# Two key loads moved from GpSimd's queue to SyncE's, and a graph part interleaved from an earlier point of an MLP

## The chip, the cores and the metric

The kernel runs on one core of a Trainium2 chip. The metric is the device time of one execution in microseconds; each kernel is run several times and the median is given. All arithmetic is in float32, apart from a small comparison buffer in bfloat16.

The engines are named as the profile names them: PE (TensorE, matmuls), PEld (its weight loads), DVE (VectorE), ACT (ScalarE), POOL (GpSimd), SP (SyncE, which here issues transfers only). "SPq" is SP's own queue of instructions. Each engine works through its instructions in order; a transfer (DMA) is issued by an engine and moves on its own afterwards.

## The reference, cut to what matters

One layer of a graph network on 1250 nodes with 768 features. A graph attention block and a linear-attention block with an MLP read the same normalized input and are added; a mixture of two chosen experts follows.

```python
xn = layernorm(x)
x = x + gnn(xn, edges) + mix(xn)            # both need xn only
x = x + ffn(layernorm(x))                   # 2 of 4 experts

def gnn(x, edges):                          # 21250 edges with the self loops
    out1 = gat(layernorm(x), W1, 4 heads)   # softmax over the edges into a node
    out2 = gat(out1, W2, 2 heads)
    return concat(x, out2) @ Wu + bu

def mix(x):
    x = x + linear_attention(layernorm(x))
    return x + gelu(layernorm(x) @ fc1) @ fc2   # 768 -> 3072 -> 768
```

## The kernel before

**The graph as a dense table.** Attention over edges is computed with a dense 1250 x 1250 table of edge counts in DRAM. There are two such tables (`tabs[0]`, `tabs[1]`), which are cleared with large transfers on SP's queue near the start (`clear`, L208). Each edge becomes a key, source times 1250 plus destination. The 21250 keys are written to DRAM (`key_d`) and taken in ten pieces of 17 columns of 125 edges. For each piece the keys are loaded again, one copy on every partition (`kr` for the first four pieces, `kr_l` for the later six), DVE compares them with the column of keys (`eq`, L295), counts duplicates (L300, L305) and computes where each count goes (`place`, L308 to L313). Then POOL issues 17 indirect transfers (L315) that add the counts into the tables, column c into `tabs[c % 2]`: 170 in all.

**The four early pieces.** They are put between the row tiles of the first matmul stage (`ps_u`, L545): piece 0 after tile 1, piece 1 after tile 3, piece 2 after tile 5, piece 3 after tile 7. `edge_piece(i)` also issues the load of piece i + 2 into one of two buffers, so that load must wait until the comparison of piece i has read its buffer. The loads of pieces 0 and 1 are issued on POOL before that stage. The later six pieces load over SP (L334).

**The stages in order of time.** Folded weights, then `ps_u` (to about 116 us), the graph's first features `ps_g` (to about 200), keys, values and queries of the linear attention (to about 440), its projection `ps_p` (L974, to about 521), then the mix MLP from about 521 to 1335, and the two experts to the end.

**The mix MLP.** It runs over 12 groups `g` of 256 hidden columns, and in each over two sets of columns `c`. The work of a group is cut in steps "P" (three matmuls of the first layer in the Strassen form, `fc1_unit`) and "h" (half a row tile of the second layer, `fc2_half`: two matmuls into a bank `ps_f`, L1077, then one DVE addition into the accumulator, L1082). There are three banks for `ps_f`. The halves done in one column set are those whose hidden values were computed in the one before. The order is written out as two strings:

```python
for c, pattern in enumerate(("PPhhhhPhhPPhhPPhhhh", "PPhhPhhPPhhPPhh")):
```

**The graph's part in the MLP.** The generator `gnn()` is the whole rest of the graph block, cut in steps that each yield a cost in us. `spend(us)` is called after each "P" (1.36 in the first column set, 2.04 in the second) and each "h" (1.39); it adds to a credit, and while the credit covers the cost of the step before, the next step is issued. What is left at the second column set of the last group is issued in one go (L1401).

The first step of `gnn()`, in `largest(4, ...)`, issues on POOL the additions of the second table to the first for the first three of ten row blocks (`merged`, L1115) and the loads of row blocks 0 and 1 of the sum (`fetch`, L1128), and yields 9.0. All of these come behind the last indirect addition into the tables. The next step begins with DVE's reading of row block 0: a `far` instruction (L1143) and then one running maximum per head (L1151 in block 0, L1147 in the others), two heads per step, cost 5.0 each. These DVE instructions are pinned (`pin`) behind what was traced before them on their engine. Unpinned instructions, such as those of the MLP, may be issued in an order other than that of the text where the program's builder finds them ready sooner.

Of the kernel before, what the change touches and what calls it, by code (L numbers as in the profile page):

```python
# [32 lines left out]
def tile_gps_layer(ctx, tc, a, out):  # L33
    nc = tc.nc
# [5 lines left out]
    def bcast(ap, p):  # L40
        return ap.partition_broadcast(p)
# [231 lines left out]
    def load_keys(i, engine):  # L273
        c0 = i * PIECE
        kr = ep.tile([128, PIECE, TP], F32, name="kr", bufs=2)
        engine.dma_start(
            kr, bcast(key_row[c0 * TP : (c0 + PIECE) * TP], 128).rearrange(
                "p (c e) -> p c e", e=TP
            ),
        )  # L280
        keys[i] = kr

    def edge_steps(i, pool, kr, parts):

        c0 = i * PIECE
        eq = pool.tile([TP, PIECE, TP], BF16, name="eq", bufs=2)
        for n in range(3):
            at = 0  # L290
            for w in parts[n]:
                cs, ks = slice(at, at + w), slice(c0 + at, c0 + at + w)
                at += w
                if n == 0:
                    pin(nc.vector.tensor_tensor(  # L295
                        eq[:, cs], kr[:TP, cs],
                        kcol[:, ks].unsqueeze(2).to_broadcast([TP, w, TP]), ALU.is_equal,
                    ))
                elif n == 1:
                    nc.vector.tensor_tensor(  # L300
                        eq[:, cs], eq[:, cs],
                        counts_of[:TP].unsqueeze(1).to_broadcast([TP, w, TP]), ALU.mult,
                    )
                else:
                    nc.vector.tensor_reduce(mult[:, ks], eq[:, cs], AX.X, ALU.add)  # L305
                yield n
        first = pool.tile([TP, PIECE], F32, name="first", bufs=2)
        nc.vector.tensor_scalar(first, mult[:, c0 : c0 + PIECE], 256.0, None, op0=ALU.is_lt)  # L308
        at = pool.tile([TP, PIECE], F32, name="at_e", bufs=2)
        nc.vector.scalar_tensor_tensor(  # L310
            at, kcol[:, c0 : c0 + PIECE], trash, first, op0=ALU.subtract, op1=ALU.mult
        )
        nc.vector.tensor_scalar(place[:, c0 : c0 + PIECE], at, trash, None, op0=ALU.add)  # L313
        for c in range(c0, c0 + PIECE):
            nc.gpsimd.indirect_dma_start(  # L315
                out=tabs[c % 2][:, :],
                out_offset=bass.IndirectOffsetOnAxis(ap=place[:, c : c + 1], axis=0),
                in_=mult[:, c : c + 1], in_offset=None,
                bounds_check=TABLE - 1, oob_is_err=True, compute_op=ALU.add,
            )  # L320

    def edge_piece(i):
        kr = keys.pop(i)
        if i + 2 < SOON:
            load_keys(i + 2, nc.gpsimd)
        for _ in edge_steps(i, ep, kr, ((PIECE,),) * 3):
            pass

# [207 lines left out]
    for t in range(NT):  # L536
        tc_ = slice(t * TP, (t + 1) * TP)
        if t + 1 < NT:
            normalized(t + 1)
        for c0, w in HALVES:  # L540
            if c0 and t + 1 < NT:
                turned_x(t + 1)
            ps = bank("ps_u")
            for k in range(KC):
                nc.tensor.matmul(  # L545
                    ps[:TP, :w], fT[:, k, tc_], wu[:, k, c0 : c0 + w],
                    start=k == 0, stop=k == KC - 1,
                )
            o = acc[:, t, c0 : c0 + w]
            nc.vector.tensor_tensor(o, ps[:TP, :w], o, ALU.add)  # L550
        for t0, n in SPLITS[1:]:
            if t == t0 - 2:
                for t1 in range(t0, t0 + n):
                    moments(acc[:, t1, :], mv[:, t1, :], vec)
                scales(t0, n)
        if t == 8:
            ahead = norms(0)
        if t in pieces:
            edge_piece(pieces[t])
# [335 lines left out]
    with tc.tile_pool(name="qp", bufs=1) as qp:  # L895
# [70 lines left out]
        for part in order2:  # L966
# [27 lines left out]
            for t in part:  # L994
                z = qp.tile([TP, D], F32, name="z2", bufs=2)
                i = where[t]
# [364 lines left out]


    steps = gnn()
    credit, cost = -44.0, 0.0

    def spend(us):
        nonlocal credit, cost
        credit += 1.05 * us
        while cost is not None and credit >= cost:
            credit -= cost  # L1370
            cost = next(steps, None)
# [15 lines left out]
    def put_half(g, c, t, j):  # L1387
        fc2_half(g, c, t, j)
        spend(1.39)
        if g == GROUPS - 1 and j:  # L1390
            last_tile(t)

    todo = []
    for g in range(GROUPS):
        if g:
            load_fc1(g + 1)
            load_fc2(g, 1)
            load_fc2(g + 1, 0)
        for c, pattern in enumerate(("PPhhhhPhhPPhhPPhhhh", "PPhhPhhPPhhPPhh")):
            if g == GROUPS - 1 and c:  # L1400
                for _ in steps:  # L1401
                    pass
                cost = None
                gnn_pool.__exit__(None, None, None)
            parts = fc1_unit(g, c)
            for p in pattern:
                if p == "P":
                    next(parts)
                    if g or c:
                        spend(2.04 if c else 1.36)  # L1410
                elif todo:
                    put_half(*todo.pop(0))
            todo = halves_of(g, c)
# [447 lines left out]
```

## Time and profile before

| | us |
|---|---|
| median of 3 runs | 1904.69 (1903.83 to 1906.24) |
| the profiled execution: its own time | 1900.13 |
| its span, first to last instruction | 1898.2 |
| PE busy | 1869.0 (98%) |
| DVE busy | 1336.0 (70%) |
| ACT busy | 803.3 (42%) |
| POOL busy | 498.0 (26%) |

PE is busy for 98% of the span, so the time is the sum of PE's work and of the few gaps in it. The shares are means over stages; where a gap lies is read from the waits of PE and from a table by stretches of time. In the timelines a line gives start, duration, engine, source line, operation, and in brackets how long the engine had been idle and what ended that.

### The profile page before, as it was taken

What the parts mean: (1) busy time and instruction counts of PE and PEld (TensorE: products, weight loads), DVE (VectorE), ACT (ScalarE), POOL (GpSimd) and SP (SyncE); (2) the same over time, 40 slices, a digit from 0 to 9 for tenths busy, and PEclk for the clock granted to TensorE, in tenths of its full rate; (3) what the DMA queues carried; (4) which work ended last, traced back from release to release, by engine and by line L of the source; (5) the groups of instructions that cost most, each with busy time, mean ns of one, the idle gap of its engine ahead of it and who ended that gap; (6) DMA issues with size and microseconds to landing.
All of it is one profiled execution on the core that took longest, in us unless ns stands there. A gap on an engine that the chain in (4) does not pass through costs nothing.

```text
span 1898.2 us, 19544 instructions
## 1 busy us (share of the span) xinstructions
PE 1869.0 (98%) x6966; PEld 1245.7 (66%) x6966; DVE 1336.0 (70%) x2407; ACT 803.3 (42%) x1207; POOL 498.0 (26%) x341
## 2 busy tenths in 40 slices
PE   9999999999998999999999999999999999999998
PEld 7555556865565668787777655566766666666664
DVE  4656692677546967676666977766677777777778
ACT  3233221331321128777674186645364353433330
POOL 2265766687882110111111121000221000000000
PEclk9999999999998999999999999999999999999999
DMA  9748532523139751233343532202485201011023
GB/s 341 238 97 213 114 85 52 134 19 49 2 30 187 136 145 55 70 95 88 106 113 79 151 111 73 69 9 67 126 101 82 71 0 67 3 64 47 12 87 109
DMA packets 184285, 175.50 MB, mean 92 GB/s; under 512 B 110043, under 2 KB 153595, under 8 KB 182908
## 3 DMA queue, kind: packets, MB, share of 16 engines
q0 software_dynamic: 126640, 68.01, 20.8%
q1 hardware_dynamic: 54270, 98.48, 16.4%
q10 hardware_dynamic: 3278, 7.75, 1.3%
q8 instruction: 55, 0.90, 0.2%
q14 instruction: 42, 0.34, 0.1%
HBM read 137.80 MB, written 42.05 MB: 95 GB/s over the span
## 4 chain that ended last, share of the span: by engine, by line
PE 91%; DMA 4%; POOL 1%; DVE 1%; issue 1%; ACT 1%; SPq 0%; DVEq 0%; POOLq 0%; ACTq 0%
PE ps_f L1077 14%; PE ps_p L81 13%; PE ps_r L81 12%; PE ps_o L1255 7%; PE ps_a L127 7%; PE ps_g L578 4%; PE ps_u L545 4%; PE ps_p L974 4%; PE ps_c L127 3%; PE ps_f L1655 3%; PE ps_o L1294 2%; PE ps_va L127 2%; PE ps_ka L127 2%; PE ps_qa L127 2%; PE ps_d L127 2%; POOL tab L315 1%
## 5 line engine op out<-in xcount | busy, mean ns | idle before, releaser
L315 POOL DMA_INDIRECT tab<-mult,place_e x170 | 351.1, 2065 | 157.7 <-DMA tab<-mult,place_e 102.6
L1077 PE MATMUL ps_f<-w,v 128*125 128x384 f32 x960 | 338.9, 487 | 6.9 <-DVE slot_a L1082 6.9
L1077 PEld LDWEIGHTS ps_f<-w,v 128*125 128x125 f32 x960 | 178.0, 188 | 113.4 <-DVE slot_a L1082 8.0
L1082 DVE TENSOR_TENSOR slot_a<-ps_f,slot_a 125x384 f32<-125x384 f32 x240 | 131.6, 553 | 66.6 <-PE ps_f L1077 62.7
L1210 DVE TENSOR_TENSOR wt<-ee 125x375 f32<-125x375 f32 (+1 forms) x180 | 105.9, 590 | 84.5 <-PE ps_o L1255 57.5
L1255 PEld LDWEIGHTS ps_o<-turns,wt 125*125 125x125 f32 x800 | 137.1, 188 | 29.1 <-DVE wt L1211 4.0
L1255 PE MATMUL ps_o<-turns,wt 125*125 125x193 f32 x800 | 151.7, 329 | 2.9 <-DVE wt L1211 2.9
L1205 ACT ACTIVATE ee<-bt,s 125x375 f32<-125x375 f32 (+1 forms) x180 | 114.8, 638 | 77.1 <-DVE wt L1210 69.8
L81 PE MATMUL ps_p<-fT,w 128*128 128x312 f32 (+1 forms) x432 | 125.5, 426 | 0.6 <-ACT c L1573 0.6
L1211 DVE SCALAR_TENSOR_TENSOR wt<-wt,slot_x 125x375 f32<-125x375 f32 (+1 forms) x180 | 105.9, 590 | 4.4
L81 PEld LDWEIGHTS ps_p<-fT,w 128*128 128x128 f32 x432 | 81.5, 189 | 36.2 <-ACT c L1573 1.1
L81 PE MATMUL ps_r<-w,slot_a 128*125 128x384 f32 x260 | 94.5, 486 | 0.0
L127 PE MATMUL ps_a<-fT,w 128*128 128x250 f32 (+1 forms) x288 | 86.8, 432 | 0.7 <-DVE slot_a L979 0.7
L1617 DVE SCALAR_TENSOR_TENSOR slot_x<-ps_r,gate,slot_x 125x384 f32<-125x384 f32 x100 | 60.7, 615 | 33.3 <-PE ps_r L81 33.0
L81 PE MATMUL ps_p<-xt,ws 128*128 128x313 f32 (+1 forms) x288 | 83.6, 426 | 0.0
L578 PE MATMUL ps_g<-fx,zT 128*125 128x388 f32 x240 | 80.2, 490 | 1.5 <-DVE zT L372 1.5
L545 PE MATMUL ps_u<-wu,fT 128*125 128x384 f32 x240 | 79.9, 487 | 0.4 <-ACT fT L531 0.4
L974 PE MATMUL ps_p<-wp,slot_x 128*125 128x384 f32 x240 | 79.9, 486 | 0.0
L1147 DVE SCALAR_TENSOR_TENSOR slot_x<-turns,s,slot_x 125x1250 f32<-125x1250 f32 x54 | 79.4, 1512 | 0.1
L1026 ACT ACTIVATE v<-v,par 128x250 f32<-128x250 f32 (+1 forms) x72 | 40.0, 556 | 88.0 <-DVE v L1046 41.3
L1208 ACT ACTIVATE ee<-bt,s1l 125x375 f32<-125x375 f32 (+1 forms) x120 | 75.4, 628 | 0.1
L81 PE MATMUL ps_r<-w2s,ht 128*125 128x384 f32 x200 | 72.7, 486 | 0.0
(403 smaller groups left out, 3413.0 us busy)
## 6 DMA issues: line engine op xcount, KB each, us to landing
turns<-g_d POOLq DMA_DIRECT2D x12, 942.4 KB, 14.2
w<-in_L_mix_fc_w_dram SPq DMA_DIRECT2D x12, 768.0 KB
w<-in_L_mix_fc_w_dram SPq DMA_DIRECT2D x24, 384.0 KB
slot_x<-tab POOLq DMA_DIRECT2D x14, 610.4 KB, 6.6
w<-in_L_ffn_w_dram SPq DMA_DIRECT2D x11, 768.0 KB
w<-in_L_ffn_w_dram SPq DMA_DIRECT2D x5, 1536.0 KB
slot_x<-tab POOLq DMA_DIRECT2D x40, 183.1 KB, 3.3
kr_l<-key_d SPq DMA_DIRECT2D x6, 1062.5 KB
```

The lines of the kernel that those rows point to most:

```text
L81: return lambda *args, **kw: pin(getattr(self.engine, name)(*args, **kw))
L127: engine.matmul(ps, wt[:, k, :], x[:, k, :], start=k == 0 and not more, stop=k == n - 1, skip_group_check=more,)
L315: nc.gpsimd.indirect_dma_start(out=tabs[c % 2][:, :], out_offset=bass.IndirectOffsetOnAxis(ap=place[:, c : c + 1], axis=0), in_=mult[:, c ...
L545: nc.tensor.matmul(ps[:TP, :w], fT[:, k, tc_], wu[:, k, c0 : c0 + w], start=k == 0, stop=k == KC - 1,)
L578: nc.tensor.matmul(ps[:TP, :388], zT[:, k, :], fx[:, k, h2 * 388 : (h2 + 1) * 388], start=k == 0, stop=k == KC - 1,)
L974: nc.tensor.matmul(ps[:TP, :w], qT[:, k, t * TP : (t + 1) * TP], pm[:, k, c0 : c0 + w], start=k == 0, stop=k == KC - 1,)
L1077: nc.tensor.matmul(ps, v_of[c][:, f, h, at : at + TP], lasts[g, j][:, f, :], start=f == 0, stop=f == 1,)
L1082: nc.vector.tensor_tensor(o, ps, o, ALU.add)
L1205: nc.scalar.activation(e[:, 0, :w], bt[:TP, 0, :w], AF.Exp, bias=s[:, 0, h, c : c + 1])
L1210: nc.vector.tensor_tensor(wt[:, :w], e[:, 0, :w], e[:, 1, :w], ALU.max)
L1211: nc.vector.scalar_tensor_tensor(wt[:, :w], wt[:, :w], 1.0, adj, op0=ALU.min, op1=ALU.mult)
L1255: nc.tensor.matmul(sums[i // 2][:TP, (i % 2) * 193 : (i % 2 + 1) * 193], wt[:, i * TP : (i + 1) * TP], gh[:, c, :], start=c == 0 and i % 2 ...
```

## The change

Two edits. The loads of pieces 2 and 3 of the keys are issued by SP instead of POOL. The credit of the interleaving begins at -20 instead of -44, and each "P" or "h" adds 1.01 times its cost instead of 1.05 times.

```diff
     def edge_piece(i):
         kr = keys.pop(i)
         if i + 2 < SOON:
-            load_keys(i + 2, nc.gpsimd)
+            load_keys(i + 2, nc.sync)
...
     steps = gnn()
-    credit, cost = -44.0, 0.0
+    credit, cost = -20.0, 0.0
 
     def spend(us):
         nonlocal credit, cost
-        credit += 1.05 * us
+        credit += 1.01 * us
         while cost is not None and credit >= cost:
             credit -= cost
             cost = next(steps, None)
```

## The prediction, made before the change was run

> **What bounds the kernel now.** I read the waits of PE first, because PE is busy 98% of the span: only its gaps can be won, and any new gap is paid in full.
>
> ```profile
> PE ps_f L1077 <- DVE slot_a L1082: 6.9, 1, 6.9
> PE ps_o L1255 <- DVE wt L1211: 2.9, 1, 2.9
> ```
>
> The largest gap lies in the mix MLP and waits for a DVE addition. The table by stretches of time (length; busy time of PE, PEld, DVE, ACT, POOL; granted clock; DMA share; GB/s) shows that the rest of the MLP has next to nothing to win:
>
> ```profile
> 580.00:600.00 20.00, 13.14 (x36) 7.33 (x35) 9.40 (x13) 1.44 (x3) 6.56 (x6) 0.78 1.22 204
> 600.00:700.00 100.00, 100.00 (x366) 65.91 (x366) 90.31 (x120) 13.80 (x28) 17.90 (x21) 0.99 0.72 141
> 700.00:720.00 20.00, 17.09 (x54) 11.15 (x53) 7.74 (x15) 13.48 (x15) 2.14 (x4) 0.91 0.41 139
> 720.00:900.00 180.00, 180.00 (x834) 144.25 (x834) 128.60 (x268) 141.71 (x208) 24.14 (x26) 1.00 0.29 79
> ```
>
> Even at 90% DVE, PE is full from 600 to 700. Next the DVE timeline around the gap, to see what the addition stood behind:
>
> ```profile
> 557.72 0.42 DVE L1046 TENSOR_TENSOR v<-ps_d,c 128x250 f32<-128x250 f32 x1 [1.71 <-PE ps_d L127]
> 558.94 0.56 DVE L1082 TENSOR_TENSOR slot_a<-ps_f,slot_a 125x384 f32<-125x384 f32 x1 [0.80 <-PE ps_f L1077]
> ...
> 579.46 0.56 DVE L1082 TENSOR_TENSOR slot_a<-ps_f,slot_a 125x384 f32<-125x384 f32 x1 [0.73 <-PE ps_f L1077]
> 590.54 0.96 DVE L1143 TENSOR_SCALAR turns<-slot_x 125x1250 f32<-125x1250 f32 x1 [10.53 <-DMA slot_x<-tab]
> 591.54 1.74 DVE L1151 TENSOR_SCALAR slot_x<-turns,s 125x1250 f32<-125x1250 f32 x2
> 593.21 0.53 DVE L1046 TENSOR_TENSOR v<-ps_d,c 128x375 f32<-128x375 f32 x1
> 593.67 1.64 DVE L1151 TENSOR_SCALAR slot_x<-turns,s 125x1250 f32<-125x1250 f32 x2
> 595.23 1.01 DVE L1082 TENSOR_TENSOR slot_a<-ps_f,slot_a 125x384 f32<-125x384 f32 x2
> ```
>
> DVE stands 10.5 us in front of the first `far` (L1143), waiting for row block 0. PE ran on until the three `ps_f` banks were full:
>
> ```profile
> 562.61 1.43 PE L127 MATMUL ps_a<-xt,ws 128*128 128x250 f32 x6
> 563.87 2.74 PE L1077 MATMUL ps_f<-w,v 128*125 128x384 f32 x8
> ...
> 587.51 1.45 PE L1077 MATMUL ps_f<-w,v 128*125 128x384 f32 x4
> 595.83 2.92 PE L1077 MATMUL ps_f<-w,v 128*125 128x384 f32 x4 [6.86 <-DVE slot_a L1082]
> 598.54 3.52 PE L127 MATMUL ps_a<-fT,w 128*128 128x375 f32 x6
> ```
>
> Last, the chain of waits, for what row block 0 itself waits for:
>
> ```profile
> 560.30 3.61 DMA tab<-mult,place_e
> 565.37 17.10 DMA tab<-tab
> 583.19 9.14 DMA slot_x<-tab
> ```
>
> The last of 170 indirect additions goes out at 560.30; then three merges and two loads follow, and the block lands at 590.5. That date hangs on POOL's additions, not on where DVE asks for it. DVE already asks too early.
>
> **Second edit: the earlier start.** Counting the costs along the two strings: the first `far` falls due when the credit covers 9.0. Before: (9 + 44) / 1.05 = 50.5 us of counted work, reached with the last "h" of group 1, column set 0 (25.4 for group 0, 26.2 for this set: 51.6). That is the addition at 579.46 above, and `far` is the very next DVE instruction, so the trace follows the text. After: (9 + 20) / 1.01 = 28.7, reached with the first "h" of the same set (25.4 + 2 x 1.36 + 1.39 = 29.5): the addition at 558.94. `far` moves 20.5 us forward in DVE's queue.
>
> With row block 0 still landing at 590.54:
> - DVE waits from 559.50 instead of 580.02: +20.5.
> - The cover shrinks. Before, PE ran on from 580.02 to 588.96 (587.51 + 1.45), 8.9 us. After, behind the first "h" stand three halves (three banks), one P (562.61) and then a half whose bank only DVE can free: PE stops at 563.87, 4.4 us after DVE. +4.5.
> - Behind `far` only two heads come before the next addition (0.96 + 1.7 = 2.7 us), where before four heads and an L1046 did (590.54 to 595.23, 4.7 us): -2.0.
>
> Sum +23.0: a PE gap of about 30 us instead of 6.9. Queued behind `far` on DVE are the additions of halves 2 to 4 and all later MLP work; PE waits for the first of them.
>
> SP's two weight loads at 566.64 and 579.45 are released by PE's progress, so they now fall behind the stall and no longer share the engines with the merges (the DMA share is 1.22 in 580 to 600). Between 0 and 3 us of gain; I take 1.5, about their share of the traffic: -1.5.
>
> **The clock after the stall.** Behind the gap four matmuls took 2.92 us instead of 1.45 and six 3.52 instead of 2.05: 2.9 us lost to the lower clock (0.78 in that stretch), in a kernel that already has it. The Trainium skill, "TensorE: Matmul & The Clock Gate", section "What's actually happening", says that the clock falls to half after an idle window of about 3.4 us and returns after one busy one, however long the idle was: 1.7 us as an estimate, against 2.9 measured. By the row the change costs nothing here, by the rule up to 1.2 us less. The row stands: 0.
>
> **What the slower rate is worth.** The generator's costs sum to 536. It ends at (536 + 44) / 1.05 = 552 before and (536 + 20) / 1.01 = 550 after, both short of the 567.6 counted before the last column set: no leftover is issued at once in either. DVE's load between falls by 4%, but PE is idle only some 3.8 us from 600 to 1335, 2.9 of it a wait for a transfer (`b_d`, then `bt`) that keeps the same steps around it. Bounds 0 to -3; I take 0.
>
> **First edit: the keys over SP.** On POOL it removes two issues:
>
> ```profile
> 52.27 0.53 POOL L276 DMA_DIRECT2D kr<-key_d  x1 [30.65 <-DVE eq L295]
> 57.18 2.12 POOL L315 DMA_INDIRECT tab<-mult,place_e  x1 [4.38 <-DVE place_e L313]
> 71.38 2.00 POOL L315 DMA_INDIRECT tab<-mult,place_e  x1 [12.08 <-DMA tab<-mult,place_e]
> ...
> 100.49 1.40 POOL L276 DMA_DIRECT2D kr<-key_d  x1
> ```
>
> The first issue lies in time in which POOL waits for `place` anyway: 0. The second frees 1.7 us (1.40 and 0.30 of issue). The first six additions, 57 to 102, wait for one another's landing while SP's loads and clears fill the engines; without a key load ahead, the first may land sooner (13.3 us after its issue, the next 11.5): -1.8.
>
> A rule of the Trainium skill speaks against more. "DMA: Bandwidth & Descriptors", section "Issuing engines are not separate DMA queues": transfers from all engines run on the same 16 DMA engines and interleave; another issuer saves only the time to initiate. By the rule the additions end 1.7 us sooner, no more. The trace can be worse: SP's key load at 179.45 is followed by additions that wait 3.10 and 3.41 us (182.36, 187.75). SP reaches the two loads behind its other loads, at 76 to 84, beside additions 2 to 5; two loads at some 3 us are +6. Against this the load at 100.49 no longer stands in front of its additions: -2. Sum -1.7 - 1.8 + 6 - 2, about 0, between -6 and +6. It moves row block 0, and so the end, one for one: from 360 on POOL issues an addition every 2.3 us almost without waits and absorbs nothing. By the rule the total would be 1.7 lower; I take 0.
>
> On SP two issues are added (0.3 us each by the `kr_l` loads). They wait for `eq` of pieces 0 and 1 (done at 52.0 and 68.7), earlier than SP gets there; behind them stands the `wk` load, which waits for PE until 116: 0. If the keys of piece 2 land late (90 to 95), DVE waits up to 6 us at 89.2 instead of 6.5 at 100.5 as now; six banks cover it, since PE is busy 83.92 of 84 us from 32 to 116. Without that cover, 6.
>
> **Sum.** 23.0 - 1.5 + 0 + 0 = +21.5 on the profiled execution's 1900.13: 1921.6. The median of the runs stands 4.6 us over that execution: 1926.2.
>
> **The rivals.**
> 1. *It is faster.* The six additions from 57 to 102 take 45 us; at 2.3 us each they would take 14. If the keys are what holds them, row block 0 lands up to 31 us sooner, DVE stands free, and the old gap goes too: -6.9 - 2.9, 1894.9. The deciding point is row block 0 at about 567: 23 us sooner it breaks even. Against it: only one of the six follows a key load; the others wait just as long. 0.05.
> 2. *`far` doesn't move as far.* MLP additions are not pinned, and the builder can let ready ones pass (L114 of the next weights ran at 553.00, before the L1046 at 557.72 that precedes it in the text). Then DVE stalls less: +3 to +14, about 1913. Against it: at 580 no ready L1046 passed `far`. 0.09.
> 3. *The keys on SP hold the additions more than counted*, 8 to 12 us: 1935 to 1939. 0.06.
>
> The rest, 0.80, is the forecast; its own range is 1917 to 1936 (scatter -6 to +6, loads and later waits -3 to +3). A difference under 0.2%, 3.8 us, can't be told from none here. Rival 1 gives faster 0.05; a little of rival 2 falls within 0.2%: same 0.04; slower 0.91. The range 1915 to 1936 leaves out rival 1, most of rival 2 and rival 3.
>
> **What the profile after would show.** Right: L1143 first waits about 30 us for `slot_x<-tab`, behind an L1082 near 559; PE's wait for L1082 is near 29 us as one gap; the last L315 is still at 554 to 567; 600 to 1335 without new waits. Wrong: the last L315 before 545 (rival 1), or L1046 and L1082 running between 560 and 590 (rival 2). A `wt` or `ee` wait grown by several us in 700 to 1335 would mean that the slower rate isn't neutral.

## The result, and the profile after

The changed kernel takes 1918.34 us, the median of 5 runs (1915.76 to 1918.56), against 1904.69 for the kernel before (5 runs, 1901.2 to 1907.02). The ratio is 1.0072 [1.0056, 1.0088]: 13.65 us slower. The profiled execution after took 1918.45 with a span of 1916.6, so the pair of profiled executions differs by 18.3. Why these two differ is taken up at the end of the explanation below.

The waits of PE after the change (total, times, longest, in us). The largest has grown from 6.9 to 32.5, in one piece. The wait at the first `ps_o` (L1255, 2.9 before) is not in the list any more; the one at L1294 is of the later two-head layer.

```profile
PE ps_f L1077 <- DVE slot_a L1082: 32.5, 1, 32.5
...
PE ps_o L1294 <- DVE wt L1211: 1.4, 2, 1.2
```

The DVE timeline after. The first `far` (L1143) now stands behind the addition at 558.87 and not behind that at 579.46, and DVE waits 35.68 us in front of it. The line after `far` is new too: an addition of the MLP, which is not pinned, comes ahead of the running maxima (L1151).

```profile
557.64 0.42 DVE L1046 TENSOR_TENSOR v<-ps_d,c 128x250 f32<-128x250 f32 x1 [1.71 <-PE ps_d L127]
558.87 0.56 DVE L1082 TENSOR_TENSOR slot_a<-ps_f,slot_a 125x384 f32<-125x384 f32 x1 [0.80 <-PE ps_f L1077]
595.10 0.88 DVE L1143 TENSOR_SCALAR turns<-slot_x 125x1250 f32<-125x1250 f32 x1 [35.68 <-DMA slot_x<-tab]
595.90 0.54 DVE L1082 TENSOR_TENSOR slot_a<-ps_f,slot_a 125x384 f32<-125x384 f32 x1
596.37 1.64 DVE L1151 TENSOR_SCALAR slot_x<-turns,s 125x1250 f32<-125x1250 f32 x2
```

The PE timeline after. PE goes on for one P (562.53) and stops near 563.97, three halves and a P behind the addition, as the count of the banks said. The first eight matmuls behind the gap take 4.48 us, where eight took 2.74 in the kernel before (563.87).

```profile
557.38 5.32 PE L1077 MATMUL ps_f<-w,v 128*125 128x384 f32 x16
562.53 1.43 PE L127 MATMUL ps_a<-xt,ws 128*128 128x250 f32 x6
596.50 4.48 PE L1077 MATMUL ps_f<-w,v 128*125 128x384 f32 x8 [32.53 <-DVE slot_a L1082]
600.81 1.43 PE L127 MATMUL ps_a<-fT,w 128*128 128x250 f32 x6
```

The chain of waits after. The last addition into the tables goes out at 564.92, before at 560.30, and the row block lands 4.6 us later (595.10 against 590.54). From one to the other it takes 30.2 us in both.

```profile
564.92 3.65 DMA tab<-mult,place_e
...
569.08 4.59 DMA tab<-tab
...
580.00 15.08 DMA slot_x<-tab
...
595.10 0.88 DVE turns L1143
```

The table by stretches after. In 560 to 600 PE is busy for 7.47 us, where it was 33.14 before. From 600 to 900 there is nothing left to win: 700 to 720 is full, where the kernel before had 17.09 of 20.

```profile
560.00:600.00 40.00, 7.47 (x21) 4.37 (x20) 4.90 (x8) 0.37 (x1) 15.68 (x12) 0.62 0.94 110
580.00:600.00 20.00, 3.50 (x6) 1.97 (x7) 4.90 (x8) 0.00 (x0) 5.09 (x5) 0.50 1.21 169
600.00:700.00 100.00, 100.00 (x368) 65.73 (x367) 92.87 (x117) 13.80 (x28) 19.06 (x21) 1.00 0.74 144
700.00:720.00 20.00, 20.00 (x79) 14.09 (x79) 10.33 (x23) 8.07 (x14) 3.07 (x5) 1.00 0.53 163
720.00:900.00 180.00, 180.00 (x823) 142.66 (x822) 126.71 (x259) 136.05 (x199) 22.51 (x23) 1.00 0.28 78
```

### The profile page after: what moved, and what is told of

Read it like the earlier page. It is cut to its first block, busy times and chain, and to the rows that moved or that the text cites. A ratio compares the mean times of both kernels' runs of the same rounds, so it can differ in the third digit from the quotient of the medians.

```text
span 1916.6 us, 19550 instructions
## 1 busy us (share of the span) xinstructions
PE 1863.1 (97%) x6966; PEld 1241.4 (65%) x6966; DVE 1338.3 (70%) x2407; ACT 806.9 (42%) x1209; POOL 496.0 (26%) x339
## 3 DMA queue, kind: packets, MB, share of 16 engines
q0 software_dynamic: 126352, 65.84, 20.5%
## 4 chain that ended last, share of the span: by engine, by line
PE 85%; POOL 5%; issue 5%; DMA 2%; DVE 1%; ACT 1%; ACTq 0%; SPq 0%; DVEq 0%; POOLq 0%
PE ps_f L1077 15%; PE ps_p L81 13%; PE ps_r L81 12%; PE ps_a L127 7%; PE ps_o L1255 7%; POOL tab L315 5%; PE ps_u L545 4%; PE ps_c L127 3%; PE ps_g L578 3%; PE ps_f L1655 3%; PE ps_o L1294 2%; PE ps_va L127 2%; PE ps_ka L127 2%; PE ps_d L127 2%; PE ps_u L1307 1%
## 5 line engine op out<-in xcount | busy, mean ns | idle before, releaser
L315 POOL DMA_INDIRECT tab<-mult,place_e x170 | 349.9, 2059 | 195.0 <-DMA tab<-mult,place_e 119.7
L1077 PE MATMUL ps_f<-w,v 128*125 128x384 f32 x960 | 339.3, 488 | 32.5 <-DVE slot_a L1082 32.5
L1082 DVE TENSOR_TENSOR slot_a<-ps_f,slot_a 125x384 f32<-125x384 f32 x240 | 132.0, 553 | 58.1 <-PE ps_f L1077 53.9
L1205 ACT ACTIVATE ee<-bt,s 125x375 f32<-125x375 f32 (+1 forms) x180 | 115.0, 639 | 90.7 <-DVE wt L1210 84.7
L1255 PEld LDWEIGHTS ps_o<-turns,wt 125*125 125x125 f32 x800 | 136.2, 187 | 25.9 <-issue 0.8
L1255 PE MATMUL ps_o<-turns,wt 125*125 125x193 f32 x800 | 149.6, 326 | 0.0
L1208 ACT ACTIVATE ee<-bt,s1l 125x375 f32<-125x375 f32 (+1 forms) x120 | 75.4, 629 | 0.1
L1026 ACT ACTIVATE v<-v,par 128x250 f32<-128x250 f32 (+1 forms) x72 | 40.0, 555 | 73.6 <-DVE v L1066 28.3
```

What stands on the lines that cost most here:

```text
L315: nc.gpsimd.indirect_dma_start(out=tabs[c % 2][:, :], out_offset=bass.IndirectOffsetOnAxis(ap=place[:, c : c + 1], axis=0), in_=mult[:, c ...
L1077: nc.tensor.matmul(ps, v_of[c][:, f, h, at : at + TP], lasts[g, j][:, f, :], start=f == 0, stop=f == 1,)
L1082: nc.vector.tensor_tensor(o, ps, o, ALU.add)
L1205: nc.scalar.activation(e[:, 0, :w], bt[:TP, 0, :w], AF.Exp, bias=s[:, 0, h, c : c + 1])
L1255: nc.tensor.matmul(sums[i // 2][:TP, (i % 2) * 193 : (i % 2 + 1) * 193], wt[:, i * TP : (i + 1) * TP], gh[:, c, :], start=c == 0 and i % 2 ...
```

## The experiments

The theory: the loss is `far` asking 20.6 us earlier for a row block whose date is set by POOL's 170 additions, and nothing else in the change matters much. The rivals: the keys on SP delay the additions; or the slower rate makes new waits later in the MLP. A second question came up on the way: what the right place for `far` is. The kernels ran on four chips, each chip with its own runs of the kernel before, and each ratio is against those. The kernel before has medians of 1897.46, 1906.61, 1906.92 and 1904.76 on the four, so a ratio from one chip is not to be compared closely with one from another.

### One edit at a time

The keys alone:

```diff
-            load_keys(i + 2, nc.gpsimd)
+            load_keys(i + 2, nc.sync)
```

> Only the keys of pieces 2 and 3 over SP; credit as before (-44, 1.05). Theory A (row block 0's landing sets when DVE may go on, and the keys on SP make the additions end later): last L315 near 565 as in the changed kernel (before: 560.3), PE's gap at L1082 about 6.9 + 4.6 = 11.5 us, time +3 to +6 over before. Theory B (the key loads are free, the later end in the changed kernel is scatter of the runs): last L315 at 558 to 562, time within 2 us of before. Theory C (POOL freed, additions end sooner): L315 before 558, time 0 to -5.

Measured: 1902.2 (22 runs), ratio 1.0018 [1.0002, 1.0033]. The profile has `far` at 593.00 behind a wait of 12.73, and a PE gap of 9.1, against 590.54, 10.53 and 6.9: the shape of the kernel before, with a table 2.5 us later and a time 3.0 longer (1903.13).

The credit alone:

```diff
-    credit, cost = -44.0, 0.0
+    credit, cost = -20.0, 0.0
...
-        credit += 1.05 * us
+        credit += 1.01 * us
```

> Only the credit (-20, 1.01); keys over POOL as before. Theory A: last L315 near 560.3, far (L1143) still right behind the L1082 at 559, DVE waits about 31 us and PE about 28 (32.5 in the changed kernel less 4.6), time +10 to +16 over before, about 4 below the changed kernel. Theory B (the keys count for nothing): the same time as the changed kernel, +13 to +15. Theory C (most of the loss comes from the keys): +0 to +5.

Measured: 1912.71 (7 runs), ratio 1.0091 [1.0057, 1.0125]. The shape of the kernel after is here without the keys, in the waits of PE and in the DVE timeline:

```profile
PE ps_f L1077 <- DVE slot_a L1082: 25.4, 1, 25.4
```
```profile
589.11 0.88 DVE L1143 TENSOR_SCALAR turns<-slot_x 125x1250 f32<-125x1250 f32 x1 [28.56 <-DMA slot_x<-tab]
```

The whole change once more, beside others on a second chip:

> The changed kernel once more, beside the kernel before and on the chip of the experiments. Theory A (the two edits add up: keys +3.4, credit +17.3 by e1_keys and e2_credit): +18 to +23 over before; PE gap 28 to 33 us. Theory H (the edits don't add; the first result holds): +11 to +16.

Measured: 1918.36 (8 runs), ratio 1.0079 [1.0048, 1.0111], as theory H had it; `far` at 594.96, PE gap 32.0, no wait at L1255.

What follows: the second edit makes the loss. (The ratios of the two edits alone multiply to 1.0109, and the whole has 1.0072 and 1.0079; the intervals are too wide to make anything of that.) The profiled executions also show what a later table costs where DVE stands waiting for it. Between the credit alone and the whole change `far` moves from 589.11 to 595.10, by 6.0 us, and the time from 1912.71 to 1918.45, by 5.7; between the kernel before and the keys alone it is 2.5 us and 3.0. One for one, nearly.

Whether the keys *make* the table later isn't settled. On the first chip the last L315 begins at 564.4 with the keys on SP and at 561.6 and 561.3 with them on POOL (the credit alone, and the later start below); on the second it is 564.6 on SP and 564.3 and 568.2 on POOL. Over all kernels with the pieces in their old places it lies in 561.8 to 564.9 with the keys on SP and in 560.3 to 568.2 on POOL. An effect of a few us of either sign hides in that scatter, and the ratio of 1.0018 just excludes zero.

The traces do say where along the 170 additions the time is lost in the pair before and after, and it is not beside the keys, which SP issues at 73 us. The 64th addition begins at 286.81 before and at 286.90 after. Two additions on, the kernel after is 6.5 us behind (4.6 are left at the end), because its 66th waits longer for an earlier one to land. First before, then after:

```profile
295.13 1.99 POOL L315 DMA_INDIRECT tab<-mult,place_e  x1 [2.17 <-DMA tab<-mult,place_e]
```
```profile
301.65 1.99 POOL L315 DMA_INDIRECT tab<-mult,place_e  x1 [8.24 <-DMA tab<-mult,place_e]
```

With the keys alone the 66th begins at 295.21, as before, and most of the delay comes behind the 118th (440.64 against 439.58; the last 564.38 against 560.30). So there is no one place for it, and what makes an addition land late there isn't shown.

### The wait taken away

If the loss is the wait for the table, it goes when the table is early. The last 34 of the 170 additions are left out, once of the kernel after and once of the kernel before. The tables then lack these edges, so the two kernels serve for their times alone:

```diff
-        for c in range(c0, c0 + PIECE):
+        for c in range(c0, c0 + PIECE) if i < 8 else ():
```

> The changed kernel, with the indirect additions of the last two pieces of edges (34 of 170) left out; all other work stays. Theory A (the earlier start costs only because the table isn't ready): the last L315 comes 34 x 2.3 = 78 us sooner, near 487, row block 0 lands near 515, far at 559 doesn't wait, no gap at 564: time 1886 to 1896, 22 to 32 us below the changed kernel. Theory E (the earlier, thinner interleaving costs by itself, by other waits in the MLP): time stays over 1900.

> The kernel before (credit -44, 1.05; keys on POOL), with the indirect additions of the last two pieces of edges left out, as in e4_cut_after. With the table early in both, the pair shows what the earlier, thinner interleaving is worth by itself. Theory F (it wins because the gap near 714 goes): 1888 to 1892, 2 to 5 us over e4_cut_after (1886). Theory G (the spread is worth nothing): within 1 us of e4_cut_after. Both: no PE gap at L1082.

Measured: 1886.13 (8 runs), ratio 0.9937 [0.9913, 0.9961] of the kernel before for the one; 1892.09 (10 runs), ratio 0.9935 [0.9914, 0.9956] for the other, on another chip. In the first `far` runs at 559.02 with no wait at all, and neither has an L1082 gap. In the table by stretches of the cut kernel after, 560 to 600 is full, and DVE does there the 36.60 us of work that it stood waiting for in the kernel after:

```profile
560.00:600.00 40.00, 40.00 (x137) 25.55 (x136) 36.60 (x43) 5.41 (x11) 10.99 (x10) 1.00 0.93 159
```

What follows: with the table out of the way the loss is gone, so the 0.7% is the wait. Whether the change is worth something besides, the ratios can't tell: 0.9937 and 0.9935 are each good to about 0.002, and the kernel before, to which they refer, differs by 9 us between the two chips. The times themselves favour the changed order: the cut kernel after is 6.0 us under the cut kernel before by the medians (on different chips) and 3.5 us by the profiles (1885.26 and 1888.75). The cut kernel before still has the wait at the first `ps_o`, and the other doesn't:

```profile
PE ps_o L1255 <- DVE wt L1211: 3.7, 1, 3.7
```

### The other way: a later start

```diff
-    credit, cost = -44.0, 0.0
+    credit, cost = -56.0, 0.0
...
-        credit += 1.05 * us
+        credit += 1.07 * us
```

> The other direction: credit -56 and rate 1.07, so that the first far falls due at (9 + 56) / 1.07 = 60.7 counted us instead of 50.5, and the generator still ends at 553 of 567.6. Theory A: DVE reaches far at about 589 to 590, when row block 0 has landed; PE's gap of 6.9 us and the slow clock behind it (2.9) go, time -5 to -10 against before if nothing new is late. Theory D (DVE, now with 2% more to do per us, becomes the bound): new waits of PE for DVE between 600 and 1335, time within 3 us of before or slower.

Measured: 1894.13 (22 runs, 1891.87 to 1897.35), ratio 0.9984 [0.9972, 0.9996]. The L1082 gap is gone from the waits of PE, and DVE does the MLP's additions until just before the row block lands:

```profile
590.01 0.56 DVE L1082 TENSOR_TENSOR slot_a<-ps_f,slot_a 125x384 f32<-125x384 f32 x1 [2.62 <-PE ps_f L1077]
592.30 0.93 DVE L1143 TENSOR_SCALAR turns<-slot_x 125x1250 f32<-125x1250 f32 x1 [1.73 <-DMA slot_x<-tab]
593.15 0.54 DVE L1082 TENSOR_TENSOR slot_a<-ps_f,slot_a 125x384 f32<-125x384 f32 x1
```

The spread tells more than the median. On the same chip the kernel before runs from 1888.5 to 1906.8 (46 runs), over 18 us, and the keys alone over 14.9 us in 22 runs; this one over 5.5 in as many, and the cut kernel after over 4.3 (8 runs). It looks as if a kernel whose DVE waits for the table hands the table's scatter on, and one that asks later doesn't.

Later still:

```diff
-    credit, cost = -44.0, 0.0
+    credit, cost = -66.0, 0.0
...
-        credit += 1.05 * us
+        credit += 1.09 * us
```

> Still later: credit -66 and rate 1.09; first far at 68.8 counted us, the end again at 552. Theory A: DVE comes to far 8 us after row block 0 has landed, nothing is won over e3_later beyond its spread: 1891 to 1896. Theory D (DVE becomes the bound as the rate grows): new PE waits for L1082 or wt between 600 and 1335, 3 to 10 us over e3_later.

Measured: 1890.43 (9 runs), ratio 0.9922 [0.9895, 0.9949], just under the times expected. In its profile the table is the latest of the kernels with the pieces in their old places (last L315 at 568.2, `far` at 600.24), and the L1082 waits are 1.1 us in all. What is left of any size in this stage is the 4.0 us at the first `ps_o`.

### The wait at the first ps_o

That wait is 2.6 to 4.0 us in every kernel so far with a start of -44, -56 or -66, and it is absent in all with -20 and 1.01. The ACT timeline of the kernel before shows what stands there: each L1026 is an activation of the MLP, each L1205 and L1208 an exponential of the graph's part, and each change from one to the other has a table load of 1.28 us ahead of it.

```profile
708.14 0.71 ACT L1205 ACTIVATE ee<-bt,s 125x500 f32<-125x500 f32 x1 [3.83 <-DMA bt<-b_d]
708.85 1.28 ACT L1026 ACT_TABLE_LOAD   x1
710.15 0.61 ACT L1026 ACTIVATE v<-v,par 128x375 f32<-128x375 f32 x1
710.76 1.28 ACT L1208 ACT_TABLE_LOAD   x1
712.05 0.71 ACT L1208 ACTIVATE ee<-bt,s1l 125x500 f32<-125x500 f32 x1
```

In the kernel after four exponentials run in a row there, with no activation of the MLP due among them:

```profile
715.05 0.71 ACT L1205 ACTIVATE ee<-bt,s 125x500 f32<-125x500 f32 x1 [3.50 <-DMA bt<-b_d]
715.67 0.69 ACT L1208 ACTIVATE ee<-bt,s1l 125x500 f32<-125x500 f32 x1
716.27 0.70 ACT L1205 ACTIVATE ee<-bt,s 125x500 f32<-125x500 f32 x1
```

The first `ps_o` matmul needs the row `bt` (loaded from `b_d`), the first two exponentials from it and two DVE instructions behind these. In the kernel before the row lands at 708.14 and the matmul begins at 714.25, 6.1 us later, because a table load, an activation of the MLP and a second table load stand between the two exponentials:

```profile
714.25 2.94 PE L1255 MATMUL ps_o<-turns,wt 125*125 125x193 f32 x8 [2.91 <-DVE wt L1211]
```

With the start of -56 nothing stands between them, and the matmul begins 2.8 us behind the row's landing (the same with -66):

```profile
707.34 0.71 ACT L1205 ACTIVATE ee<-bt,s 125x500 f32<-125x500 f32 x1 [3.02 <-DMA bt<-b_d]
707.96 0.69 ACT L1208 ACTIVATE ee<-bt,s1l 125x500 f32<-125x500 f32 x1
```
```profile
710.13 2.93 PE L1255 MATMUL ps_o<-turns,wt 125*125 125x193 f32 x8 [2.59 <-DVE wt L1211]
```

So the wait has two causes. In the kernel before it is the table loads: 2.8 us behind its row would have been 710.9, before PE ran out of work at 711.34 (an estimate from these lines). With -56 and -66 it is the row itself, which lands too late for the work that PE has in hand.

The next experiment keeps the later start of -56 and puts six empty steps of 2.5 counted us, not four, between the store of `b_d` and the first exponential, which gives PE more MLP work while the row travels:

```diff
-        yield from rest(4)
+        yield from rest(6)
...
-    credit, cost = -44.0, 0.0
+    credit, cost = -56.0, 0.0
...
-        credit += 1.05 * us
+        credit += 1.07 * us
```

> e3_later (credit -56, rate 1.07) with rest(6) instead of rest(4) behind the store of the row b_d, 5.0 more counted us of MLP work before the first exponentials. Theory I (the waits at the first ps_o, 2.6 and 3.2 us in e3_later, are the store and load of b_d and bt): both go, with the slow clock behind them: 4 to 8 us below e3_later, 1886 to 1890. Theory J (they are ACT's table loads between the GELU and the exponential, whatever the cover): within 2 us of e3_later (1894).

Measured: 1889.77 (10 runs), ratio 0.9924 [0.9901, 0.9946]; the wait at L1255 is gone, L1294 is at 1.0, and the L1082 waits are three small ones:

```profile
PE ps_f L1077 <- DVE slot_a L1082: 3.1, 3, 1.5
```

That is theory I: more cover for the row takes the wait away. The time alone does not show what the two steps are worth: on the same chip the start of -66 without them has 1890.43, the same within the noise, and the start of -56 without them (1894.13) ran on another chip.

Its `far` runs at 595.14, the date of the kernel after within 0.04 us: at equal tables the two profiled executions are 1888.31 and 1918.45, 30.1 us apart, and their L1082 waits 3.1 and 32.5.

The same kernel on a third chip, with more to compare:

> e8_rest once more, beside the two others: 10 to 17 us below before by theory I, as in the first run of it (0.9924); 1887 to 1892 if the chip's own times are like those.

Measured: 1889.24 (6 runs), ratio 0.9901 [0.9885, 0.9917]. This version beats both kernels: 0.8 to 1.0% under the one before on these two chips. On the first chip, where the kernel before has 1897.46, the same 1889.5 would be 0.4% under it (an estimate): the gain depends on how late the table falls in the kernel before.

### Starting the additions sooner

If the table is late, one may start it earlier: the four early pieces one row tile sooner.

```diff
-    pieces = {1: 0, 3: 1, 5: 2, 7: 3}
+    pieces = {0: 0, 2: 1, 4: 2, 6: 3}
```

> The kernel before with the four early pieces each one row tile sooner (after tiles 0, 2, 4, 6), credit as before. Theory A (the table's date sets before's gap): the first L315 near 49 instead of 57; the first six still wait for one another, the last ends 5 to 10 us sooner (551 to 556), the gap at L1082 goes wholly or nearly; time -5 to -10 against before, with the wait at the first ps_o left. Theory K (SP's clears and loads until about 88 hold the early additions anyway): the last L315 at 558 to 562 and the time within 3 us of before.

Measured: 1908.79 (12 runs), ratio 1.0006 [0.999, 1.0022]. The POOL timeline has the first additions at 50.45 and 63.85, where the kernel before has 57.18 and 71.38:

```profile
50.45 2.13 POOL L315 DMA_INDIRECT tab<-mult,place_e  x1 [5.75 <-DVE slot_a L550]
63.85 2.01 POOL L315 DMA_INDIRECT tab<-mult,place_e  x1 [11.27 <-DMA tab<-mult,place_e]
```

By about the 69th addition the lead is gone (312.0 against 308.2), the last begins at 563.5, and the wait at `ps_g` has grown from 1.5 us to 6.8. The earlier pieces with a start between the two and the six empty steps:

```diff
-    pieces = {1: 0, 3: 1, 5: 2, 7: 3}
+    pieces = {0: 0, 2: 1, 4: 2, 6: 3}
...
-        yield from rest(4)
+        yield from rest(6)
...
-    credit, cost = -44.0, 0.0
+    credit, cost = -48.0, 0.0
...
-        credit += 1.05 * us
+        credit += 1.06 * us
```

> e9_pieces and e8_rest together, with credit -48 and rate 1.06 (first far at 53.8 counted us, end at 560 of 567.6). Theory A: no gap at L1082, no wait at the first ps_o: 1884 to 1889, 1 to 4 us below e8_rest. Theory K: a gap of 3 to 6 us at L1082, time 2 to 6 us over e8_rest.

Measured: 1902.01 (12 runs), ratio 0.997 [0.9954, 0.9985], some 12 us over the version without the earlier pieces, which neither theory foresaw. The last addition begins at 570.5 in its profile, the latest of all, and `far` waits 10.6 us for the table. What follows: the date of the table isn't set by when the additions begin.

### The rate

The kernel after with the old rate (`-` is the kernel after here):

```diff
-        credit += 1.01 * us
+        credit += 1.05 * us
```

> The changed kernel with the old rate (1.05) and the new start (-20): far falls due at (9 + 20) / 1.05 = 27.6 counted us, behind the same first h as with 1.01 (29.5); the generator ends at 529.5. Theory L (the slower rate as such is worth nothing): PE's gap at L1082 again 30 to 33 us, time within 3 us of the changed kernel, +12 to +18 over before; a wait at the first ps_o may or may not come back, since its place against the strings is another. Theory M (the slower rate relieves DVE): new PE waits for DVE between 600 and 900, 4 us or more over the changed kernel.

That expectation rests on a miscount of mine: with 1.05 the credit after the second P is (25.4 + 2 x 1.36) x 1.05 - 20 = 9.5 and covers the 9.0 already, so `far` comes one "h" earlier, ahead of the L1046 as well. The DVE timeline shows it:

```profile
556.32 0.55 DVE L1082 TENSOR_TENSOR slot_a<-ps_f,slot_a 125x384 f32<-125x384 f32 x1
590.92 1.15 DVE L1143 TENSOR_SCALAR turns<-slot_x 125x1250 f32<-125x1250 f32 x1 [34.05 <-DMA slot_x<-tab]
592.10 1.65 DVE L1151 TENSOR_SCALAR slot_x<-turns,s 125x1250 f32<-125x1250 f32 x2
593.67 0.41 DVE L1046 TENSOR_TENSOR v<-ps_d,c 128x250 f32<-128x250 f32 x1
```

Measured: 1931.77 (4 runs), ratio 1.0149 [1.0126, 1.0172]. The gap is 32.3 us although the table is 4.2 us earlier than in the kernel after, and the waits of PE have two more that the kernel after hasn't. (PE waits for an activation of the MLP here, because the L1046 that feeds it stands behind `far`.)

```profile
PE ps_f L1077 <- ACT v L1026: 32.3, 1, 32.3
...
PE ps_c L127 <- DVE ws L114: 2.8, 1, 2.8
...
PE ps_o L1255 <- DVE wt L1211: 2.0, 1, 2.0
```

Place and rate changed together here, so how much of the further loss belongs to which stays open. It does say that 1.01 against 1.05 isn't what makes the changed kernel slow.

## Why the prediction was right, and where its sum was off

The forecast was 1926.2 with a range of 1915 to 1936. The measured 1918.34 lies in the range, near its lower end, and 7.9 below the forecast. The mechanism is the one predicted: `far` behind the first "h" of group 1, one gap, near 30 us. By the steps:

- **The move of `far`, +20.5.** DVE's wait begins at 559.42 in place of 580.01: 20.6.
- **The smaller cover, +4.5.** PE stops 4.55 us after DVE, where it was 8.95: +4.4.
- **Behind `far`, -2.0.** Mis-sized. From `far` to the first matmul it takes 1.4 us, where it took 5.3: -3.9. I had let both heads' L1151 precede the addition, since these are pinned; the addition isn't, and ran at 595.90, ahead of them. The prediction named such passing as rival 2 (ahead of `far`); it happened one instruction later.
- **The keys 0, SP's loads -1.5.** In this pair the table is 4.6 us later; nothing came sooner. From the last addition to `far` it is 30.2 us in both kernels, so the relief from the two weight loads, which was argued from their share of the traffic, isn't there. The +6 for two key loads beside the additions was of the right kind: the fifth addition is at 99.94 and was at 95.41. But the chain takes that back (the 21st is at 147.1, and was at 147.3), so it is not this lag that makes the table later: the time is lost behind the 64th. SP took 3.02 us to issue the two loads, not 0.3 each.
- **The clock, 0.** Here the row was the wrong guide. Before, ten matmuls lost 2.9 us behind a gap of 6.9; after, the eight behind a gap of 32.5 lost 4.48 - 2.74 = 1.74, and the six that followed ran at the full speed (1.43). The rule of the Trainium skill, "TensorE: Matmul & The Clock Gate", section "What's actually happening" (one busy window of about 3.4 us returns the clock, however long the idle was), gave 1.7 as an estimate and so -1.2, which is what came. The same section says that the window runs freely, so the loss depends on where in a window the work begins again; two gaps with 2.9 and 1.7 agree with that, but no run here separates it.
- **The slower rate, 0 with bounds 0 and -3.** Below the bounds in this pair: the wait at the first `ps_o` (2.91) and the slow matmuls behind it (2.94 for eight that take 1.47) are gone, -4.4. I had called it a wait for a transfer that "keeps the same steps around it". Neither holds: in the kernel before it was the alternation of table loads on ACT, and a different rate and start let the exponentials fall between other activations. Near 1335 to 1360 the clock is at half for 3.4 us instead of 6.8, about -1.7 more. This part isn't the rate's: the keys alone, with the old rate, have the same mean clock from 1325 to 1380 as the kernel after (0.97; the kernel before has 0.94).

The sum for the profiled pair: 20.6 + 4.4 - 3.9 + 4.6 = 25.7, the growth of the gap; less 1.2, 4.4 and 1.7 it is 18.4, the difference of the spans. The 4.6 in it is the later table, which the prediction's sum held fixed at 590.54. Without it the steps come to 13.8, where 21.5 were predicted: 7.7 too much, nearly all of the 7.9.

**The term that was mis-sized most is the slower rate:** -6.1 in place of 0, of which 1.7 isn't the rate's doing; and whether the rate or the start took the wait at the first `ps_o` away was not separated. "Behind `far`" and the clock took 1.9 and 1.2 more off, and SP's loads gave nothing where 1.5 had been counted. The 23 us of the early request itself were right to within 2.

**The last step, +4.6, came in, but I didn't know what it was.** I carried the distance of the median from the profiled execution over to the other side. The one-for-one pairs of profiles suggest what it is: the profiled execution before was one in which the table was early (590.54), and there every us of the table is about a us of the time. With the table at 595.10 the kernel before would take 1900.13 + 4.6 = 1904.7 (an estimate), and 1904.69 is its median. The profiled execution after has its table at 595.10 and lies at its own median (1918.45 and 1918.34). Then the forecast with the measured steps is 1900.13 + 13.8 + 4.6 = 1918.5, as measured; and 18.3 and 13.65 differ because the profiled pair has the 4.6 us of the table in it and the pair of medians hasn't. In the runs without a profile the table's date can't be seen, so this account fits the numbers and isn't shown.

The rivals: the table did not come 23 us sooner (rival 1), `far` moved all of its way (rival 2), and the keys on SP did not hold the additions for 8 to 12 us (rival 3; 4.6 in this pair, inside the scatter).

## What to carry to other kernels

Before moving the consumer of a late result, find the date of that result and who sets it: an in-order engine that asks early blocks all that is queued behind it, and here 20 us earlier cost 0.7%, where a request 10 to 18 counted us later gained from 0.2% to 1.0%, by the chip and by what came with it. A profiled execution is one draw: where the path hangs on a chain that scatters, bring both sides to the same date of it before comparing them, and prefer an order that leaves slack, which narrowed the spread here as well. When two streams of work share an engine with function tables, their phase matters: a wait that seems to be for a transfer can be the tables going back and forth. The same line in the list of waits can have another cause in the next kernel, so read the engine's timeline in each.

## What the runs showed of the hardware

- A chain of 170 indirect additions, each some 2.3 us on POOL (1.99 and 0.30 of issue), ends anywhere from 560.3 to 568.2 in kernels that differ only behind it, and an earlier start by 6.7 us left nothing of itself at the end. A single addition that waited 8.24 us for an earlier one, where it had waited 2.17, made most of the difference in the pair before and after.
- SP's two broadcast key loads took 3.02 us to issue among its other loads, where 0.3 each had been taken from the later ones.
- The lower clock cost 2.9 and 2.8 us behind gaps of 6.9 and 9.1 us (the kernel before, the keys alone), and 2.2, 2.0 and 1.7 us behind gaps of 25.4, 32.0 and 32.5 us (the credit alone, the whole change twice): in these runs a longer stall cost no more clock.
- ACT's table load is 1.28 us, and the kernel before has six of them from 708 to 720. Two of them between the first two exponentials put the first `ps_o` 6.1 us behind the landing of its row, where it is 2.8 us without them.
